# Ordering a four-direction scan kernel by pairs of units: one joined ssm_out, W ahead of the projections, c*h on GpSimd

## The chip, the cores and the metric

One core of a Trainium2 chip runs the whole program. The metric is the device time of one execution in microseconds (us). The engines are named as the profile names them: PE is TensorE's matmuls, PEld its weight loads, DVE VectorE, ACT ScalarE, POOL GpSimd.

## The reference, cut to what matters

An image batch (4, 128, 96, 96) is normalised by groups, read in four directions (rows, columns, each forwards and backwards), and each direction runs this block in fp32:

```python
t = _grouped1x1(x, in_proj_w, in_proj_b, G)
u, gate = (t[:, :HID], t[:, HID:])
u = jax.nn.silu(u)
u = lax.conv_general_dilated(u, dw_w, ...)          # depthwise, 5 taps
s = _conv1x1(u, ssm_in_w)
a = DMIN + (DMAX - DMIN) * jax.nn.sigmoid(_conv1x1(u, ssm_delta_w, ssm_delta_b))
a = jnp.clip(a, 0.0001, 0.9999)
bb = jnp.tanh(_conv1x1(u, ssm_b_w, ssm_b_b))
cc = jnp.tanh(_conv1x1(u, ssm_c_w, ssm_c_b))
prefix = jnp.cumsum(jnp.log(a), axis=-1)
hst = jnp.exp(prefix) * jnp.cumsum(bb * s * jnp.exp(-prefix), axis=-1)
u = u + _conv1x1(cc * hst + ssm_d[None, :, None] * s, ssm_out_w)
u = _grouped1x1(u * jax.nn.sigmoid(gate), mix_w, mix_b, G)
return _conv1x1(u, out_proj_w, out_proj_b)          # then the fuse of four directions, x +
```

The kernel computes `hst` as a first-order scan h = a*h + b*s. It folds mix, out_proj and fuse into one matrix, called W below.

## The kernel before

A *unit* is 384 positions of one stream; the two streams (a direction and its reverse) alternate, so two consecutive units are a *pair*. There are 384 units, 192 pairs. The last stages of a unit run 12 units behind its first ones. The names used below: *rows* are the in-projection matmuls (front `pf` and gate `pg`), *conv* `pc`, *projections* `pp`, *ssm_out* `pz`, *W* `py`. Two more names occur in the profiles: `gv` is the tile that W reads, and *gating* the two VectorE instructions that make it out of ssm_out and the gate; *bn_stats* collects the statistics of the next image.

```python
banks = []
w, x, y, z, h = range(5)
for _ in range(NU // 2 + 16):                      # PSUM banks rotate from unit to unit
    banks.append({"f": (w, x), "g": (y, z), "y": y, "c": (z, None), "t": h})
    banks.append({"f": (w, x), "g": (z, y), "y": h, "c": (z, y), "t": None})
    w, x, y, z, h = x, h, z, y, w
# ... in rows(), behind the 16 front and gate matmuls of a unit:
pz = ps.tile([P, 2, 512], F32, tag="z", name=f"pz_{bu['id']}")
for c in range(4):
    for j in range(2):                             # 8 tiles of 32x32: this unit's stream alone
        r = slice(64 * j + 32 * bu["s"], 64 * j + 32 * bu["s"] + 32)
        mm(pz[:, j, :], c, w_so[r, ...], z[r, bu["p"], :], True, True)
# ...
def outputs(step, p):
    ta, tb = scans[step]
    nc.vector.tensor_mul(tb[0:64, p, :], tb[0:64, p, :], ta[0:64, p, :])     # c*h
    nc.vector.tensor_add(tb[64:P, p, :], tb[0:64, p, :], tb[64:P, p, :])     # z
    nc.gpsimd.tensor_copy(tb[0:64, p, :], tb[64:P, p, :])                    # its copy
# ... the order on TensorE within unit(t):
#   rows (16 tiles), ssm_out (8), W of the unit before, conv (1 or 2), projections
```

Of the kernel before, what the change touches and what calls it, by code (L numbers as in the profile page):

```python
# [48 lines left out]
LAG = 12  # L49
# [4 lines left out]
def conv_preact_kernel(  # L54
# [58 lines left out]
    def psb(bank, name):  # L113
        return ps.tile([P, 512], F32, tag=f"bank{bank}", name=name)



    banks = []
    w, x, y, z, h = range(5)
    for _ in range(NU // 2 + 16):  # L120
        banks.append({"f": (w, x), "g": (y, z), "y": y, "c": (z, None), "t": h})
        banks.append({"f": (w, x), "g": (z, y), "y": h, "c": (z, y), "t": None})
        w, x, y, z, h = x, h, z, y, w
# [39 lines left out]
    def stats_finish(b):  # L163
# [4 lines left out]
        pm = ps.tile([P, 512], F32, tag="p", name=f"pm_{b}")  # L168
# [10 lines left out]
        pv = ps.tile([P, 512], F32, tag="p", name=f"pv_{b}")  # L179
# [7 lines left out]
        pb = ps.tile([P, 512], F32, tag="p", name=f"pbn_{b}")  # L187
# [65 lines left out]
    with tc.tile_pool(name="prep", bufs=1) as pp:  # L253
# [31 lines left out]
        for d in range(4):  # L285
            for j in range(2):
                pt = psb(2 * (d % 2) + j, f"pof_{d}_{j}")
                nc.tensor.matmul(
                    pt[:, :P], w_out[:, bass.ts(j, P)], w_fuse[:, d, :], start=True, stop=True
                )  # L290
                nc.scalar.copy(w_of[:, d, j, :], pt[:, :P])
        for d in range(4):
            for j in range(2):
                pt = psb(2 * (d % 2) + j, f"pfin_{d}_{j}")
# [4 lines left out]
        pb = psb(4, "pb")  # L299
# [21 lines left out]
    def gating(bu):  # L321
        gv = bu["v"]
        nc.vector.scalar_tensor_tensor(gv, gv, 1.0, bu["pz"][:, :, :N], ALU.add, ALU.mult)  # L323

# [5 lines left out]
    def rows(i, bi, bk):  # L330

        front = gate = None
        if i is not None:
# [9 lines left out]
            pf = [psb(bk["f"][j], f"pf_{i}_{j}") for j in range(2)]  # L343
            front = (un, wn, bsil, s, g, sil, pf)
        if bi is not None:
            bu = units[bi]
            gwn, gbn, _ = stats[bu["b"]]
            pg = [psb(bk["g"][j], f"pg_{bu['id']}_{j}") for j in range(2)]
            gate = (bu, gwn, gbn, pg)
        so = bu["s"] if gate else 0  # L350
        for e in (so, 1 - so):
            r, rg = slice(32 * e, 32 * e + 32), slice(64 + 32 * e, 96 + 32 * e)
            for c in range(4):
                if front:
                    m, q = (c, g) if by_taps(s, e) else (g, c)
                    mm(pf[e], c, wn[r, 32 * m : 32 * m + 32], x_in[s][r, q, :], True, True)
                if gate:
                    q, off = gate_at(bu)
                    mm(pg[e], c, gwn[rg, 32 * c : 32 * c + 32],
                       x_in[bu["s"]][rg, q, off : off + N], True, True)  # L360
        if gate:
            pz = ps.tile([P, 2, 512], F32, tag="z", name=f"pz_{bu['id']}")
            z = scans[bu["step"]][1]
            for c in range(4):
                for j in range(2):
                    r = slice(64 * j + 32 * bu["s"], 64 * j + 32 * bu["s"] + 32)
                    mm(pz[:, j, :], c, w_so[r, 128 * j + 32 * c : 128 * j + 32 * c + 32],
                       z[r, bu["p"], :], True, True)
        if gate:
            gv = wk.tile([P, 2, N], F32, tag="gv", name=f"gv_{bu['id']}")  # L370
            for j in range(2):
                nc.scalar.activation(  # L372
                    gv[:, j, :], pg[j][:, :N], AF.Tanh, bias=gbn[:, 2 + j : 3 + j], scale=0.5
                )
            load_gate(bi + UB)
            nc.vector.tensor_add(pz[:, :, :N], pz[:, :, :N], bu["u"])  # L376
            bu["pz"], bu["v"] = pz, gv
        if front:
            for j in range(2):
                nc.scalar.activation(  # L380
                    sil[:, j, g, :],
                    pf[j][:, : N + 1],
# [3 lines left out]
            if g == 3:  # L386
                for j in range(2):
                    if un["st"] == 0:
# [18 lines left out]
    def taps(un, ks, bk):  # L407
        sil, j = sils[un["step"], un["s"]], 1
        if 0 in ks:
            un["pt"] = psb(bk["t"], f"pt_{un['id']}")  # L410
# [229 lines left out]
```

## Time and profile before

| | before |
|---|---|
| median of 3 runs | 2586.16 us (2585.37 to 2586.33) |
| busy PE, DVE, ACT, POOL | 98%, 78%, 60%, 20% of 2589.8 us |
| one pair in mid-kernel | 12.90 us, 36 slots of 0.3225 us and 1.29 us of other time |
| ahead of the first ssm_out, and from the last one's start to the end | 99.9 and 10.4 us |

Read the busy shares as a list of engines that cannot be the bound, not as a measure of TensorE. PE's 98% includes time in which tiles drain or start late, and those 1.29 us per pair are as much a target as the slots are. The lines that carry this are in the prediction.

### The profile page before, as it was taken

To read this page: it belongs to the slowest core of one execution; us is meant where nothing else is said; L and a number is where in the kernel's file an instruction comes from. 1 tells how busy PE (TensorE), PEld (TensorE's weight loads), DVE (VectorE), ACT (ScalarE), POOL (GpSimd) and SP (SyncE) were. 2 spreads that over 40 slices of the span, in tenths; PEclk is the share of its full clock that TensorE was granted. 3 is DMA by queue.
4 is the path that set the end of the run, shared out by engine and by line. 5 is a ranking of instruction groups with operands and counts; after the bars stand their busy time and mean duration, and the time that the engine had idled before them with its cause. 6 is when DMAs were issued, how large, how long until landed. Compare 5 with 4: busy or idle time off the path is not lost.

```text
span 2589.8 us, 89224 instructions
## 1 busy us (share of the span) xinstructions
PE 2534.8 (98%) x40016; PEld 964.0 (37%) x40016; DVE 2023.1 (78%) x2727; ACT 1554.8 (60%) x2912; POOL 512.2 (20%) x786
## 2 busy tenths in 40 slices
PE   6999999999999999999999999999999999999997
PEld 3333333333333333333333333333333333333332
DVE  3688878877878887877887887777887788778876
ACT  4666666666656666666665666666666666666652
POOL 4211121111111112111111111211111111111110
PEclk8999999999999999999999999999999999999999
DMA  5112111112332111111232211111133111111111
GB/s 141 46 45 51 45 37 30 36 30 84 94 92 51 45 48 28 36 30 36 81 112 81 51 45 31 36 30 36 30 101 110 36 30 36 29 36 30 29 42 58
DMA packets 79278, 134.18 MB, mean 52 GB/s; under 512 B 11440, under 2 KB 73392, under 8 KB 78896
## 3 DMA queue, kind: packets, MB, share of 16 engines
q1 hardware_dynamic: 76704, 127.64, 18.4%
q8 instruction: 315, 5.16, 0.8%
q10 hardware_dynamic: 2192, 0.83, 0.1%
q14 instruction: 67, 0.55, 0.1%
HBM read 109.55 MB, written 18.87 MB: 50 GB/s over the span
## 4 chain that ended last, share of the span: by engine, by line
PE 95%; DVE 1%; ACT 1%; DMA 1%; issue 0%; DVEq 0%; ACTq 0%
PE pc L317 29%; PE py L317 21%; PE pp L317 20%; PE pz L317 12%; PE pf L317 11%; PE pg L317 2%; DVE gv L323 0%; DVE t L479 0%; DMA out<-acc 0%; ACT t L445 0%; DMA acc<-in_xr 0%; ACT gv L372 0%; DMA x_in<-in_xs 0%; ACT L445 0%; ACT L182 0%
## 5 line engine op out<-in xcount | busy, mean ns | idle before, releaser
L317 PE MATMUL pc<-sil,band 128*32 128x384 f32 x9216 | 822.1, 489 | 0.3 <-ACT gv L372 0.3
L402 ACT COPY u<-pc 128x384 f32<-128x384 f32 x576 | 276.2, 479 | 568.3 <-PE pc L317 567.0
L317 PE MATMUL pp<-u,w_proj 128*32 128x384 f32 x6144 | 596.0, 489 | 7.1 <-ACT std L182 5.6
L317 PE MATMUL py<-gv,w_fin 128*32 128x384 f32 x6144 | 580.0, 495 | 6.2 <-ACT gv L372 4.2
L417 DVE SCALAR_TENSOR_TENSOR pt<-sil,w_tap,pt 128x384 f32<-128x384 f32 x576 | 358.5, 622 | 180.9 <-ACT pt L415 165.8
L317 PEld LDWEIGHTS pc<-sil,band 128*32 128x32 f32 x9216 | 297.4, 110 | 457.6 <-issue 388.9
L372 ACT ACTIVATE gv<-pg,bnorm 128x384 f32<-128x384 f32 x768 | 403.1, 576 | 97.3 <-PE pg L317 97.3
L317 PE MATMUL pz<-t,w_so 32*32 32x384 f32 x6144 | 430.7, 492 | 5.6 <-DVE gv L323 5.5
L459 DVE TENSOR_TENSOR t<-pp,t 64x384 f32<-64x384 f32 x192 | 176.2, 918 | 286.9 <-ACT t L451 286.8
L376 DVE TENSOR_TENSOR pz<-pz,u 128x768 f32<-128x768 f32 x384 | 369.8, 963 | 14.4 <-PE pz L317 8.5
L317 PE MATMUL pf<-x_in,wn 32*32 32x385 f32 x6144 | 362.6, 504 | 8.2 <-DVE acc L504 7.2
L317 PE MATMUL pg<-x_in,wn 32*32 32x384 f32 x6144 | 360.2, 494 | 3.4 <-DVE acc L511 3.4
L323 DVE SCALAR_TENSOR_TENSOR gv<-gv,pz 128x768 f32<-128x768 f32 x384 | 362.6, 944 | 0.1
L448 POOL TENSOR_SCALAR t<-t 64x384 f32<-64x384 f32 x192 | 184.0, 958 | 858.9 <-ACT t L445 858.9
L317 PEld LDWEIGHTS pp<-u,w_proj 128*32 128x32 f32 x6144 | 224.7, 109 | 304.4 <-issue 259.8
L487 POOL COPY t<-t 64x384 f32<-64x384 f32 x192 | 96.3, 501 | 1156.7 <-DVE t L486 1156.7
L380 ACT ACTIVATE sil<-pf,bsilu 128x385 f32<-128x385 f32 x576 | 314.6, 586 | 3.9 <-PE pf L317 3.3
L317 PEld LDWEIGHTS py<-gv,w_fin 128*32 128x32 f32 x6144 | 160.7, 109 | 397.1 <-issue 270.2
L451 ACT ACTIVATE t<-pp,b_proj 64x384 f32<-64x384 f32 x192 | 110.6, 576 | 242.6 <-PE pp L317 122.4
L445 ACT ACTIVATE t<-pp,b_proj 128x384 f32<-128x384 f32 x192 | 187.0, 974 | 70.2 <-PE pp L317 53.8
L317 PEld LDWEIGHTS pz<-t,w_so 32*32 32x32 f32 x6144 | 167.1, 103 | 165.2 <-issue 91.7
L449 POOL TENSOR_SCALAR t<-t 64x384 f32<-64x384 f32 x192 | 184.8, 962 | 15.9
(65 smaller groups left out, 1474.0 us busy)
## 6 DMA issues: line engine op xcount, KB each, us to landing
x_in<-in_xs SPq DMA_DIRECT2D x96, 385.0 KB, 4.3
x_in<-in_xs SPq DMA_DIRECT2D x384, 96.2 KB, 2.4
out<-acc SPq DMA_DIRECT2D x24, 768.0 KB, 3.6
xs<-in_xr SPq DMA_DIRECT2D x72, 192.0 KB, 2.4
acc<-in_xr SPq DMA_DIRECT2D x18, 768.0 KB, 4.7
acc<-in_xr SPq DMA_DIRECT2D x24, 192.0 KB, 3.6
w_fuse<-in_fuse_wT ACTq DMA_DIRECT2D x1, 256.0 KB, 4.9
w_proj<-in_proj_wT ACTq DMA_DIRECT2D x1, 128.0 KB, 4.6
```

What stands on the lines that cost most here:

```text
L317: nc.tensor.matmul(o[r, : rhs.shape[-1]], lhsT, rhs, start=start, stop=stop, skip_group_check=True)
L323: nc.vector.scalar_tensor_tensor(gv, gv, 1.0, bu["pz"][:, :, :N], ALU.add, ALU.mult)
L372: nc.scalar.activation(gv[:, j, :], pg[j][:, :N], AF.Tanh, bias=gbn[:, 2 + j : 3 + j], scale=0.5)
L376: nc.vector.tensor_add(pz[:, :, :N], pz[:, :, :N], bu["u"])
L380: nc.scalar.activation(sil[:, j, g, :], pf[j][:, : N + 1], AF.Silu, bias=bn[:, j : j + 1] if by_taps(s, j) else bsil[:, j, g : g + 1],)
L402: nc.scalar.copy(un["u"][:, j, :], pc[:, :N])
L417: nc.vector.scalar_tensor_tensor(un["u"][:, j, :] if k == K - 1 else part, src, w_tap[:, k : k + 1], part, ALU.mult, ALU.add,)
L445: nc.scalar.activation(ta[:, p, :], pp[:, :N], AF.Tanh, bias=b_proj[:, 0:1])
L448: nc.gpsimd.tensor_scalar(a, a, half, DMIN + half, ALU.mult, ALU.add)
L449: nc.gpsimd.tensor_scalar(a, a, 0.9999, 0.0001, ALU.min, ALU.max)
L451: nc.scalar.activation(tb[0:64, p, :], pp[0:64, :N], AF.Tanh, bias=b_proj[0:64, 1:2])
L459: nc.vector.tensor_mul(ta[0:64, p, :], pp[64:P, :N], ta[0:64, p, :])
```

## The change

The intent: the 32x32 matmuls of ssm_out used two of the four row groups of the array, one stream at a time. Taking both streams of a pair together fills all four. To make that possible all work is ordered by pairs, PSUM banks become fixed, W of the even unit moves between convolution and projections, and c*h and z go to GpSimd. The diff cut to its core:

```diff
-    for _ in range(NU // 2 + 16):
-        banks.append({"f": (w, x), "g": (y, z), "y": y, "c": (z, None), "t": h})
...
+    psum = ps.tile([P, 8, 512], F32, name="psum")
+    GATE, FRONT, CONV_R, Y_F, SMALL = (0, 1), (2, 3), (0, 1), 2, 3
+    SSM, PROJ, Y_R, CONV_F = (4, 6), (5, 4), 6, 7
...
+    def ssm_out(bi):
+        pair = units[bi], units[bi + 1]
+        z, p = scans[pair[0]["step"]][1], pair[0]["p"]
+        for c in range(4):
+            for s in range(2):
+                for j in range(2):
+                    r = slice(64 * j + 32 * s, 64 * j + 32 * s + 32)
+                    mm(bank(SSM[s] + j), c, w_so[r, ...], z[r, p, :], True, True)
+        for s, bu in enumerate(pair):
+            pz, gv = psum[:, SSM[s] : SSM[s] + 2, :N], bu["v"]
+            nc.vector.tensor_add(pz, pz, bu["u"])
+            nc.vector.scalar_tensor_tensor(gv, gv, 1.0, pz, ALU.add, ALU.mult)
...
-        nc.vector.tensor_mul(tb[0:64, p, :], tb[0:64, p, :], ta[0:64, p, :])
-        nc.vector.tensor_add(tb[64:P, p, :], tb[0:64, p, :], tb[64:P, p, :])
+        nc.gpsimd.tensor_mul(ta[64:P, p, :], tb[0:64, p, :], ta[0:64, p, :])
+        nc.gpsimd.tensor_add(tb[64:P, p, :], ta[64:P, p, :], tb[64:P, p, :])
         nc.gpsimd.tensor_copy(tb[0:64, p, :], tb[64:P, p, :])
...
+    def pair(t):             # order on TensorE, shortened
+        inputs(i - 2); rows(front, bi); accumulate(units[bi - 1]); conv(units[i], 0)
+        scan(...); outputs(...)
+        rows(front + 1, bi + 1); ssm_out(bi); conv(units[i + 1], 0 and 1)
+        accumulate(units[bi]); taps(units[i + 2], range(K)); proj(i, 1); proj(i, 0)
```

`accumulate` is W. `inputs` is the tanh of the first projection, GpSimd's two clamping operations and the product b*s. The taps, the convolution of one half of the channels done on VectorE, now accumulate in u itself instead of a PSUM bank.

More of the change, by code (lines that the diff above doesn't have):

```diff
@@ L48 @@
 M = WW // R
-LAG = 12
+LAG = 6
 UB = 8
@@ L111, in conv_preact_kernel, with bank @@
     NU = len(units)
-    def psb(bank, name):
-        return ps.tile([P, 512], F32, tag=f"bank{bank}", name=name)
-    banks = []
-    w, x, y, z, h = range(5)
-    for _ in range(NU // 2 + 16):
-        banks.append({"f": (w, x), "g": (y, z), "y": y, "c": (z, None), "t": h})
-        banks.append({"f": (w, x), "g": (z, y), "y": h, "c": (z, y), "t": None})
-        w, x, y, z, h = x, h, z, y, w
+    psum = ps.tile([P, 8, 512], F32, name="psum")
+    GATE, FRONT, CONV_R, Y_F, SMALL = (0, 1), (2, 3), (0, 1), 2, 3
+    SSM, PROJ, Y_R, CONV_F = (4, 6), (5, 4), 6, 7
+    def bank(i):
+        return psum[:, i, :]
     gmean = wp.tile([P, P], F32, name="gmean")
@@ L167, in stats_finish @@
         yield
-        pm = ps.tile([P, 512], F32, tag="p", name=f"pm_{b}")
+        pm = bank(SMALL)
         nc.tensor.matmul(pm[:, 0:1], gmean, mv[:, 0:1], start=True, stop=True)
@@ L178, in stats_finish @@
         yield
-        pv = ps.tile([P, 512], F32, tag="p", name=f"pv_{b}")
+        pv = bank(SMALL)
         nc.tensor.matmul(pv[:, 0:1], gmean, ex, start=True, stop=True)
@@ L186, in stats_finish @@
         yield
-        pb = ps.tile([P, 512], F32, tag="p", name=f"pbn_{b}")
+        pb = bank(SMALL)
         nc.tensor.matmul(pb[:, 0:4], wn, gm4, start=True, stop=True)
@@ L286, in conv_preact_kernel @@
             for j in range(2):
-                pt = psb(2 * (d % 2) + j, f"pof_{d}_{j}")
+                pt = bank(2 * (d % 4) + j)
                 nc.tensor.matmul(
@@ L293, in conv_preact_kernel @@
             for j in range(2):
-                pt = psb(2 * (d % 2) + j, f"pfin_{d}_{j}")
+                pt = bank(2 * (d % 4) + j)
                 nc.tensor.matmul(
@@ L298, in conv_preact_kernel @@
                 nc.scalar.mul(w_fin[:, d, j, :], pt[:, :P], 0.5)
-        pb = psb(4, "pb")
+        pb = bank(0)
         terms = [(w_of[:, d, j, :], b_mix[:, j : j + 1]) for d in range(4) for j in range(2)]
@@ L318, in mm @@
                          skip_group_check=True)
-    def gating(bu):
-        gv = bu["v"]
-        nc.vector.scalar_tensor_tensor(gv, gv, 1.0, bu["pz"][:, :, :N], ALU.add, ALU.mult)
     def by_taps(s, j):
@@ L328, in conv_preact_kernel, with rows @@
     sils = {}
-    def rows(i, bi, bk):
-        front = gate = None
+    def rows(i, bi, front_banks=FRONT):
         if i is not None:
@@ L342, in rows @@
             sil = sils[step, s]
-            pf = [psb(bk["f"][j], f"pf_{i}_{j}") for j in range(2)]
-            front = (un, wn, bsil, s, g, sil, pf)
         if bi is not None:
@@ L347, in rows @@
             gwn, gbn, _ = stats[bu["b"]]
-            pg = [psb(bk["g"][j], f"pg_{bu['id']}_{j}") for j in range(2)]
-            gate = (bu, gwn, gbn, pg)
-        so = bu["s"] if gate else 0
-        for e in (so, 1 - so):
-            r, rg = slice(32 * e, 32 * e + 32), slice(64 + 32 * e, 96 + 32 * e)
-            for c in range(4):
-                if front:
-                    m, q = (c, g) if by_taps(s, e) else (g, c)
-                    mm(pf[e], c, wn[r, 32 * m : 32 * m + 32], x_in[s][r, q, :], True, True)
-                if gate:
-                    q, off = gate_at(bu)
-                    mm(pg[e], c, gwn[rg, 32 * c : 32 * c + 32],
-                       x_in[bu["s"]][rg, q, off : off + N], True, True)
-        if gate:
-            pz = ps.tile([P, 2, 512], F32, tag="z", name=f"pz_{bu['id']}")
-            z = scans[bu["step"]][1]
-            for c in range(4):
-                for j in range(2):
-                    r = slice(64 * j + 32 * bu["s"], 64 * j + 32 * bu["s"] + 32)
-                    mm(pz[:, j, :], c, w_so[r, 128 * j + 32 * c : 128 * j + 32 * c + 32],
-                       z[r, bu["p"], :], True, True)
-        if gate:
+            gq, off = gate_at(bu)
+        for c in range(4):
+            for j in range(2):
+                if i is not None:
+                    r = slice(32 * j, 32 * j + 32)
+                    m, q = (c, g) if by_taps(s, j) else (g, c)
+                    mm(bank(front_banks[j]), c, wn[r, 32 * m : 32 * m + 32], x_in[s][r, q, :],
+                       True, True)
+                if bi is not None:
+                    r = slice(64 + 32 * j, 96 + 32 * j)
+                    mm(bank(GATE[j]), c, gwn[r, 32 * c : 32 * c + 32],
+                       x_in[bu["s"]][r, gq, off : off + N], True, True)
+        if bi is not None:
             gv = wk.tile([P, 2, N], F32, tag="gv", name=f"gv_{bu['id']}")
@@ L372, in rows @@
                 nc.scalar.activation(
-                    gv[:, j, :], pg[j][:, :N], AF.Tanh, bias=gbn[:, 2 + j : 3 + j], scale=0.5
+                    gv[:, j, :],
+                    bank(GATE[j])[:, :N],
+                    AF.Tanh,
+                    bias=gbn[:, 2 + j : 3 + j],
+                    scale=0.5,
                 )
             load_gate(bi + UB)
-            nc.vector.tensor_add(pz[:, :, :N], pz[:, :, :N], bu["u"])
-            bu["pz"], bu["v"] = pz, gv
-        if front:
+            bu["v"] = gv
+        if i is not None:
             for j in range(2):
@@ L381, in rows @@
                     sil[:, j, g, :],
-                    pf[j][:, : N + 1],
+                    bank(front_banks[j])[:, : N + 1],
                     AF.Silu,
@@ L387, in rows, with conv @@
                 for j in range(2):
+                    tap = by_taps(s, j)
                     if un["st"] == 0:
-                        r = (slice(0, P), slice(0, 2)) if by_taps(s, j) else (slice(0, 64), slice(0, 4))
-                        nc.gpsimd.memset(sil[r[0], j, r[1], 0:1], 0.0)
+                        r, q = (slice(0, P), slice(0, 2)) if tap else (slice(0, 64), slice(0, 4))
+                        nc.gpsimd.memset(sil[r, j, q, 0:1], 0.0)
                     if un["st"] == NS - 1:
-                        r = (slice(0, P), slice(2, 4)) if by_taps(s, j) else (slice(64, P), slice(0, 4))
-                        nc.gpsimd.memset(sil[r[0], j, r[1], N : N + 1], 0.0)
+                        r, q = (slice(0, P), slice(2, 4)) if tap else (slice(64, P), slice(0, 4))
+                        nc.gpsimd.memset(sil[r, j, q, N : N + 1], 0.0)
                 load_front(step + 1, s)
-    def conv(un, j, bk):
+    def ssm_out(bi):
+        pair = units[bi], units[bi + 1]
+        z, p = scans[pair[0]["step"]][1], pair[0]["p"]
+        for c in range(4):
+            for s in range(2):
+                for j in range(2):
+                    r = slice(64 * j + 32 * s, 64 * j + 32 * s + 32)
+                    mm(bank(SSM[s] + j), c, w_so[r, 128 * j + 32 * c : 128 * j + 32 * c + 32],
+                       z[r, p, :], True, True)
+        for s, bu in enumerate(pair):
+            pz, gv = psum[:, SSM[s] : SSM[s] + 2, :N], bu["v"]
+            nc.vector.tensor_add(pz, pz, bu["u"])
+            nc.vector.scalar_tensor_tensor(gv, gv, 1.0, pz, ALU.add, ALU.mult)
+    def conv(un, j):
         sil = sils[un["step"], un["s"]]
-        pc = psb(bk["c"][j], f"pc_{un['id']}_{j}")
+        pc = bank(CONV_R[j] if un["s"] else CONV_F)
         for k in range(2):
@@ L404, in new_u, with taps @@
     def new_u(un):
-        un["u"] = wk.tile([P, 2, N], F32, tag="u", bufs=LAG + 1, name=f"u_{un['id']}")
-    def taps(un, ks, bk):
+        un["u"] = wk.tile([P, 2, N], F32, tag="u", bufs=2 * LAG + 2, name=f"u_{un['id']}")
+    def taps(un, ks):
         sil, j = sils[un["step"], un["s"]], 1
-        if 0 in ks:
-            un["pt"] = psb(bk["t"], f"pt_{un['id']}")
         for k in ks:
             off, q = divmod(un["p"] + k, R)
-            src, part = sil[:, j, q, off : off + N], un["pt"][:, :N]
+            src, part = sil[:, j, q, off : off + N], un["u"][:, j, :]
             if k == 0:
@@ L417, in taps @@
                 nc.vector.scalar_tensor_tensor(
-                    un["u"][:, j, :] if k == K - 1 else part,
-                    src,
-                    w_tap[:, k : k + 1],
-                    part,
-                    ALU.mult,
-                    ALU.add,
+                    part, src, w_tap[:, k : k + 1], part, ALU.mult, ALU.add
                 )
@@ L435, in proj @@
                 wk.tile([P, N, R], F32, tag="t0", name=f"t0_{step}").rearrange("p n r -> p r n"),
-                wk.tile([P, R, N], F32, tag="t1", name=f"t1_{step}"),
+                wk.tile([P, R, N], F32, tag="t1", bufs=3, name=f"t1_{step}"),
             ]
         ta, tb = scans[step]
-        pp = ps.tile([P, 512], F32, tag="p", name=f"pp_{un['id']}_{which}")
+        pp = bank(PROJ[which])
         cols = (qb, qb, qa, qa) if which == 0 else (qc, qc, qs, qs)
@@ L443, in proj @@
                 mm(pp, c, w_proj[:, j, cols[c]], units[i + c % 2]["u"][:, j, :], j == 0, j == 1)
-        if which == 0:
-            nc.scalar.activation(ta[:, p, :], pp[:, :N], AF.Tanh, bias=b_proj[:, 0:1])
-            a = ta[64:P, p, :]
-            half = (DMAX - DMIN) / 2
-            nc.gpsimd.tensor_scalar(a, a, half, DMIN + half, ALU.mult, ALU.add)
-            nc.gpsimd.tensor_scalar(a, a, 0.9999, 0.0001, ALU.min, ALU.max)
-        else:
+        if which == 1:
             nc.scalar.activation(
@@ L453, in proj, with inputs @@
             )
-            un["pp"] = pp
-    def products(i):
+            nc.scalar.activation(tb[64:P, p, :], pp[64:P, :N], AF.Copy, scale=d_sb[64:P, :])
+    def inputs(i):
         un = units[i]
-        (ta, tb), p, pp = scans[un["step"]], un["p"], un["pp"]
-        nc.vector.tensor_mul(ta[0:64, p, :], pp[64:P, :N], ta[0:64, p, :])
-    def skip(i):
-        un = units[i]
-        tb = scans[un["step"]][1]
-        nc.scalar.activation(
-            tb[64:P, un["p"], :], un["pp"][64:P, :N], AF.Copy, scale=d_sb[64:P, :]
-        )
+        ta, p = scans[un["step"]][0], un["p"]
+        nc.scalar.activation(ta[:, p, :], bank(PROJ[0])[:, :N], AF.Tanh, bias=b_proj[:, 0:1])
+        a = ta[64:P, p, :]
+        half = (DMAX - DMIN) / 2
+        nc.gpsimd.tensor_scalar(a, a, half, DMIN + half, ALU.mult, ALU.add)
+        nc.gpsimd.tensor_scalar(a, a, 0.9999, 0.0001, ALU.min, ALU.max)
+        nc.vector.tensor_mul(ta[0:64, p, :], bank(PROJ[1])[64:P, :N], ta[0:64, p, :])
     def scan(step, part):
@@ L484, in outputs, with accumulate @@
         ta, tb = scans[step]
-        nc.vector.tensor_mul(tb[0:64, p, :], tb[0:64, p, :], ta[0:64, p, :])
-        nc.vector.tensor_add(tb[64:P, p, :], tb[0:64, p, :], tb[64:P, p, :])
+        nc.gpsimd.tensor_mul(ta[64:P, p, :], tb[0:64, p, :], ta[0:64, p, :])
+        nc.gpsimd.tensor_add(tb[64:P, p, :], ta[64:P, p, :], tb[64:P, p, :])
         nc.gpsimd.tensor_copy(tb[0:64, p, :], tb[64:P, p, :])
-    def accumulate(bu, bk):
+    def accumulate(bu):
         b, s, p, st = bu["b"], bu["s"], bu["p"], bu["st"]
-        py = psb(bk["y"], f"py_{bu['id']}")
+        py = bank(Y_R if s else Y_F)
         for j in range(2):
@@ L519, in conv_preact_kernel @@
     later = []
-    def unit(t):
-        bi, k, bk = t - LAG, t % UB, banks[t]
-        un = units[t] if t < NU else None
-        if t % 2 and 0 <= t - 3 < NU:
-            products(t - 3)
-        if t % 2 and 0 <= t - 11 < NU:
-            d = units[t - 11]
-            outputs(d["step"], d["p"])
-        if un and k % 2 == 0:
-            taps(un, range(1, K), bk)
-        rows(t + UB if t + UB < NU else None, bi if 0 <= bi < NU else None, bk)
-        if t % 2 and 0 <= t - 3 < NU:
-            skip(t - 3)
-        if 0 <= bi - 1 < NU:
-            accumulate(units[bi - 1], bk)
-        if 0 <= bi < NU:
-            gating(units[bi])
-        if un:
-            conv(un, 0, bk)
-            if k % 2:
-                conv(un, 1, bk)
+    def pair(t):
+        i, k, bi = 2 * t, t % R, 2 * (t - LAG)
+        conv_here = i < NU
+        front = i + UB if i + UB < NU else None
+        back = 0 <= bi < NU
+        if 0 <= i - 2 < NU:
+            inputs(i - 2)
+        rows(front, bi if back else None)
+        if 0 <= bi - 2 < NU:
+            accumulate(units[bi - 1])
+        if conv_here:
+            conv(units[i], 0)
+        if k < 2 and 0 <= t // R - 1 < NU // UB:
+            scan(t // R - 1, k)
+        if 0 <= i - 10 < NU:
+            d = units[i - 10]
+            outputs(d["step"], d["p"])
+        if conv_here:
+            un = units[i]
+            if un["order"] == "V" and un["b"] + 1 < B:
+                stats_chunk(un["b"] + 1, un["st"] * R + k)
+                if un["st"] == NS - 1 and k == R - 1:
+                    later[:] = [stats_finish(un["b"] + 1)]
+        if front is not None or back:
+            rows(None if front is None else front + 1, bi + 1 if back else None)
+        if back:
+            ssm_out(bi)
+        if conv_here:
+            new_u(units[i + 1])
+            for j in range(2):
+                conv(units[i + 1], j)
+        if back:
+            accumulate(units[bi])
@@ L542, in unit @@
         if later:
             next(later[0], None)
-        if un and un["order"] == "V" and k % 2 == 0 and un["b"] + 1 < B:
-            stats_chunk(un["b"] + 1, (un["st"] * UB + k) // 2)
-            if un["st"] == NS - 1 and k == UB - 2:
-                later[:] = [stats_finish(un["b"] + 1)]
-        if k in (1, 2) and 0 <= t // UB - 1 < NU // UB:
-            scan(t // UB - 1, k - 1)
-        if t + 1 < NU:
-            new_u(units[t + 1])
-            if k % 2:
-                taps(units[t + 1], [0], banks[t + 1])
@@ L554, in unit @@
-        if k % 2 and un:
-            proj(t - 1, 0)
-        elif k % 2 == 0 and 2 <= t <= NU:
-            proj(t - 2, 1)
+        if i + 2 < NU:
+            new_u(units[i + 2])
+            taps(units[i + 2], range(K))
+        if conv_here:
+            proj(i, 1)
+            proj(i, 0)
     for _ in stats_finish(b0):
@@ L561, in conv_preact_kernel @@
     for i in range(UB):
-        r = 2 * (i % 2)
-        rows(i, None, {"f": (r, r + 1)})
+        rows(i, None, (2 * (i % 2), 2 * (i % 2) + 1))
     new_u(units[0])
-    taps(units[0], [0], banks[0])
+    taps(units[0], range(K))
     with tc.manual_schedule(
@@ L568, in conv_preact_kernel @@
     ):
-        for t in range(NU + LAG + 1):
-            unit(t)
+        for t in range(NU // 2 + LAG + 1):
+            pair(t)
 _NAMES = [
```

## The prediction

> **What bounds the kernel now.** I read the page's busy times first, then the chain of work that ended last, then the groups of lines, and only then the timeline, because "98% busy" on TensorE does not say whether its time is streaming, switching or waiting.
>
> ```profile
> PE 2534.8 (98%) x40016; PEld 964.0 (37%) x40016; DVE 2023.1 (78%) x2727; ACT 1554.8 (60%) x2912; POOL 512.2 (20%) x786
> ...
> PE pc L317 29%; PE py L317 21%; PE pp L317 20%; PE pz L317 12%; PE pf L317 11%; PE pg L317 2%; DVE gv L323 0%; DVE t L479 0%; DMA out<-acc 0%; ACT t L445 0%; DMA acc<-in_xr 0%; ACT gv L372 0%; DMA x_in<-in_xs 0%; ACT L445 0%; ACT L182 0%
> ...
> L317 PE MATMUL pz<-t,w_so 32*32 32x384 f32 x6144 | 430.7, 492 | 5.6 <-DVE gv L323 5.5
> L376 DVE TENSOR_TENSOR pz<-pz,u 128x768 f32<-128x768 f32 x384 | 369.8, 963 | 14.4 <-PE pz L317 8.5
> L317 PE MATMUL pf<-x_in,wn 32*32 32x385 f32 x6144 | 362.6, 504 | 8.2 <-DVE acc L504 7.2
> ```
>
> The chain is matmuls from end to end: TensorE's own order sets the time, and no other engine is above 78%. The counts show that each fp32 matmul is recorded as two passes (6144 = 192 pairs x 16 matmuls x 2). The timeline of TensorE's weight loads in mid-kernel shows how a pass is paced:
>
> ```profile
> 1304.47 0.11 PEld L317 LDWEIGHTS pp<-u,w_proj 128*32 128x32 f32 x1 [0.19 <-issue]
> 1304.79 0.28 PEld L317 LDWEIGHTS pp<-u,w_proj 128*32 128x32 f32 x7 [0.21 <-issue]
> ...
> 1306.05 0.10 PEld L317 LDWEIGHTS pz<-t,w_so 32*32 32x32 f32 x1
> 1306.37 0.42 PEld L317 LDWEIGHTS pz<-t,w_so 32*32 32x32 f32 x15 [0.22 <-issue]
> 1307.42 0.16 PEld L317 LDWEIGHTS py<-gv,w_fin 128*32 128x32 f32 x8 [0.62 <-ACT gv L372]
> 1307.77 0.13 PEld L317 LDWEIGHTS py<-gv,w_fin 128*32 128x32 f32 x4 [0.19 <-issue]
> 1308.09 0.13 PEld L317 LDWEIGHTS py<-gv,w_fin 128*32 128x32 f32 x4 [0.19 <-issue]
> 1308.41 0.13 PEld L317 LDWEIGHTS pc<-sil,band 128*32 128x32 f32 x4 [0.19 <-issue]
> ```
>
> Four column tiles start together and the next four follow 0.323 us later. I call that a slot; a slot costs the same whether 4, 8 or 16 tiles share it. The matmul rows of the same stretch:
>
> ```profile
> 1304.14 1.63 PE L317 MATMUL pp<-u,w_proj 128*32 128x384 f32 x16
> 1305.70 0.51 PE L317 MATMUL pf<-x_in,wn 32*32 32x385 f32 x1
> 1305.70 0.51 PE L317 MATMUL pg<-x_in,wn 32*32 32x384 f32 x1
> ...
> 1306.15 0.48 PE L317 MATMUL pg<-x_in,wn 32*32 32x384 f32 x1
> 1306.37 1.12 PE L317 MATMUL pz<-t,w_so 32*32 32x384 f32 x16
> 1307.42 1.50 PE L317 MATMUL py<-gv,w_fin 128*32 128x384 f32 x16
> ```
>
> pz (ssm_out) ends at 1307.49, so its last matmul of 0.48 started at 1307.01 and W (py) came 0.41 later. pp's last start (1305.28) to pf is 0.42. So a change between 32-row and 128-row tiles costs 0.41 after the last start, about 0.09 more than a slot. And pz occupies 1306.37 to 1307.42, 1.05 us for two slots of work (0.65): its first tile starts on time, the other loads come later and spread.
>
> Two units repeat every 12.90 us: rows start at 1305.70, 1311.43 and 1318.60 (5.73 + 7.17). Slots in that: conv 12, projections 8, W 8, pz 4, rows 4 = 36, times 0.3225 = 11.61. The other 1.29 us: two rows-pz-W passages at 0.40 each, two entries to rows 0.11 and 0.27, two rows passes 0.03 each. The 0.27 comes from the odd unit's projection, one load at 1304.79 while the rest wait for ScalarE's copy of u.
>
> **What the Trainium skill says.** "TensorEngine Tiling (Array Packing)", Key Properties, says that a change of tiling mode drains TensorE; the trace agrees, 0.41 us from last start to first start. Its table of 32x32 tiles has 16 positions; old pz uses 8 at a time, rows use 16 at the price of one slot. "GPSIMD Engine Reference", 3.1, gives a GpSimd tensor_tensor of 2048 fp32 4497 ns, and section 7 adds half for steps over 8 bytes. No GpSimd tensor_tensor is in this trace. "SBUF — State Buffer", Who interferes with whom, says a VectorE instruction with two SBUF inputs contends with GpSimd reads. The trace shows it:
>
> ```profile
> 353.52 1.81 DVE L479 TENSOR_TENSOR_SCAN t<-t 64x768 f32<-64x768 f32 x1
> 353.59 5.46 POOL L195 COPY bsilu<-bnorm 32x2 f32<-32x2 f32 x15
> ```
>
> These copies have a mean of 284 ns; 15 of them are 4.3 us, but took 5.46 beside the scan.
>
> **The change, part by part, per pair of units on TensorE.**
>
> 1. ssm_out once per pair on all four row groups: 4 slots become 2. Removed 2 x 0.3225 = 0.645. This is not all gain: rows to pz to W now occurs once. Today it takes 1.37 us from the rows' second pass to W, twice = 2.74. After, the first rows of the pair go straight to W: 16 starts spread over 0.10, then 0.41 = 0.51. The second rows go to ssm_out with 16 tiles instead of 8. The trace's loads of pz fill 0.42 us for 15, of which the second part is spread at about 17 ns a tile; eight more tiles add 0.13, so 1.37 + 0.13 = 1.50. Sum 2.01: saved 0.73. If the tiles go out at the rows' rate (7 ns) it is 1.36 and the saving 0.87.
> 2. W of the even unit between convolution and projections: 4 slots = 1.29 us in which ScalarE's copy (0.48) finishes. The stall of the odd projection goes: 0.27 - 0.11 = 0.16.
> 3. The number of mode changes stays four per pair (rows to W, conv to rows, ssm_out to conv, projection to rows).
>
> Sum 0.73 + 0.16 = 0.89, with the favourable rate 1.03; by adding up afresh: 34 slots = 10.97, rows 0.05, rows to W 0.19, rows to ssm_out to conv 0.53, two entries 0.22 = 11.96 (or 11.82). I take 11.93. 192 pairs x (12.90 - 11.93) = 186 us.
>
> 4. c*h and z leave VectorE: 192 x (909 + 555 ns) = 281 us, 1.46 per pair. VectorE falls from about 2023 to 1742, 9.1 of 11.9 us per pair. It is not on the chain, so this buys only slack, but slack that is needed: both gatings now come together after one ssm_out.
> 5. GpSimd gains 192 x 2 operations. Estimate from the skill's page: 4497/2048 = 2.2 ns x 384 = 0.84, half more for the strided scan tile = 1.26 us each. 512 + 192 x 2.5 = 992 us, 5 of 11.9 us per pair: no bound. A pair's z is made one pair before ssm_out reads it.
> 6. Taps accumulate in u (SBUF) instead of PSUM. The same 622 ns expected.
>
> **Do the other engines keep up?** From the start R of a pair's first rows: ScalarE's tanh starts 0.13 after R (1305.83), gate tanh at 0.98, Silu at 1.92, done 2.98 (1308.68). The second rows need those banks at 0.84 + W 1.29 + conv 1.29 + 0.11 = R + 3.53; margin 0.5. ssm_out ends near R + 5.4. VectorE then needs 0.99 + 0.86 (starts at 1303.36, 1304.35; 1304.89, 1305.75) for the first gating, so gv is ready at 7.4; W wants it at 5.35 + 8 slots = 7.93. Margin 0.5. The second gating is done at 9.3, W of it is due at 12.8. Taps (4 x 0.64) after the accumulation end at about 12.6, 0.7 into the next pair; its products at 1.1 to 2.1, accumulation to 2.9, and where there is a scan, GpSimd's clamps end at 3.2 and the scan at 5.0, before ssm_out's end.
>
> Head, tail and batch changes: 2589.8 - 192 x 12.90 = 113 us. Same lag (12 units = 6 pairs), same reloads of the accumulator, so I leave them, less a few us in the head.
>
> **Rivals.** (a) VectorE becomes late in the pairs with a scan: GpSimd starts c*h just when the scan wants the shared read port, the scan waits up to 1.3 us, gating slips past the 0.5 us margin, and TensorE waits for gv. One pair in four, up to 0.8 us: 48 x 0.8 = 38 us, total about 2440. For it: bsilu's case above; against it: the ordering lets the scan start second only by 0.1 us, and most pairs have slack. (b) Fixed PSUM banks take the place of rotation: bank 2 serves rows and even W, banks 0 and 1 gate and convolution. Any lateness of ScalarE or VectorE then stops rows at once. A loss of 0.5 us in each pair makes 2500. Against: every margin I found is 0.2 us or more, and the waits show ScalarE's copy of u waiting 567 us in all for TensorE, not the reverse. (c) The passage into 16 tiles of ssm_out is no cheaper than two of 8, as starts are issued serially: then only parts 2 and the single drain remain, 0.3 us per pair, about 2530. The rows' 16 starts within 0.11 us speak against it. (d) GpSimd so slow that z comes late: it would need over 5 us more per pair than estimated.
>
> **Range and chances.** 2586 - 186 = 2400, plus about 8 us for scan pairs (a quarter of rival a): 2408 us. Low end: 7 ns rate and shorter tail, 2586 - 1.09 x 192 = 2377, less a little. High end: rivals a and a part of b, 2465. Faster by over 2% is below 2534: only rival c in full or b with two thirds of a microsecond per pair prevents it. Faster 0.94, within 2% 0.05, slower 0.01.
>
> **What would show it.** Right: TensorE still over 95% busy, rows repeating every 11.8 to 12.0 us per pair, ssm_out's busy time near 192 x 1.25 = 240 us instead of 431 (its 1.12 per unit plus 0.13 for the wider set, once per pair), no wait of TensorE on ScalarE in the projections, VectorE near 1740 us, GpSimd near 1000. Wrong: periods alternating with the scan pairs, W waiting for VectorE's gv, rows waiting for Silu or for acc, or ssm_out lasting over 1.3 us.

## The result, and the profile after

| | before | after |
|---|---|---|
| median, 4 runs each | 2586.24 us | 2461.41 us (2459.89 to 2466.89) |
| ratio | | 0.9522, 95% interval 0.9505 to 0.9538 |
| busy PE, DVE, ACT, POOL in us | 2535, 2023, 1555, 512 | 2389, 1859, 1573, 1051 |

A ratio here is the mean time of one kernel's fast runs over the mean of the other's of the same rounds, so it is not quite the ratio of the medians. The change is faster by 4.8%. The time lies inside the predicted range, 53 us above its centre.

The page of the changed kernel, with the lines that answer to those of before. All matmul outputs are now called psum, so the stage is read from the inputs: t is ssm_out, gv is W, x_in the rows. The numbers behind the bar are busy us, mean ns, and idle time ahead with what ended it.

```profile
PE psum L314 82%; DVE t L465 4%; ACT t L447 2%; DVE gv L394 2%; DVE psum L393 2%; POOL t L450 1%; POOL t L451 1%; DVE u L415 0%; DMA out<-acc 0%; DVE bn L310 0%; DMA acc<-in_xr 0%; ACT gv L353 0%; ACT L364 0%; ACT L438 0%; ACT sil L364 0%
...
L314 PE MATMUL psum<-gv,w_fin 128*32 128x384 f32 x6144 | 582.9, 497 | 31.0 <-DVE gv L394 29.0
...
L472 POOL TENSOR_TENSOR t<-t,t 64x384 f32<-64x384 f32 x192 | 289.1, 1506 | 15.0
L471 POOL TENSOR_TENSOR t<-t,t 64x384 f32<-64x384 f32 x192 | 249.5, 1300 | 95.9 <-DVE t L465 85.9
L314 PE MATMUL psum<-t,w_so 32*32 32x384 f32 x6144 | 256.2, 493 | 2.9 <-DVE t L452 2.9
```

Three things stand in it. ssm_out went from 430.7 us to 256.2, near the 240 expected. The chain is no longer TensorE from end to end: 4% of it is the scan (L465), and the two gating lines (L393, L394) and GpSimd's clamps are in it too. And W now waits for gv, 29 us by this count.

TensorE's timeline in the changed kernel, one whole pair without a wait (columns: start, duration, engine, line, operation):

```profile
1326.67 0.94 PE L314 MATMUL psum<-x_in,wn 32*32 32x385 f32 x32
1327.54 1.51 PE L314 MATMUL psum<-gv,w_fin 128*32 128x384 f32 x16
1328.85 1.49 PE L314 MATMUL psum<-sil,band 128*32 128x384 f32 x16
1330.27 0.93 PE L314 MATMUL psum<-x_in,wn 32*32 32x385 f32 x32
1330.94 1.30 PE L314 MATMUL psum<-t,w_so 32*32 32x384 f32 x32
1332.17 2.79 PE L314 MATMUL psum<-sil,band 128*32 128x384 f32 x32
1334.78 1.47 PE L314 MATMUL psum<-gv,w_fin 128*32 128x384 f32 x16
1336.07 2.77 PE L314 MATMUL psum<-u,w_proj 128*32 128x384 f32 x32
1338.76 0.94 PE L314 MATMUL psum<-x_in,wn 32*32 32x385 f32 x32
```

Subtract starts, not ends: ends are modelled and overlap. Rows to rows is 1338.76 - 1326.67 = 12.09 us against 12.90. The first rows reach W in 0.87, the second rows pass ssm_out and reach the convolution in 1.90: 2.77, where the kernel before needed 2 x 1.72 = 3.44. Projections to rows is 2.69, 8 slots and 0.11.

But one pair in four is longer. The starts of ssm_out put the pairs at a median of 12.06 to 12.09 us, except those that hold the first half of a scan, at 12.52 (mean 12.60, some at 12.97). Here is one of the longest kind on TensorE:

```profile
1319.19 2.79 PE L314 MATMUL psum<-sil,band 128*32 128x384 f32 x32
1322.66 1.50 PE L314 MATMUL psum<-gv,w_fin 128*32 128x384 f32 x16 [0.69 <-DVE gv L394]
```

The conv takes 2.61 us without a wait; here W starts 3.47 after it, because gv is not there. VectorE and GpSimd at that time:

```profile
1317.06 2.93 DVE L465 TENSOR_TENSOR_SCAN t<-t,t 64x768 f32<-64x768 f32 x1 [0.36 <-POOL t L451]
1320.03 0.56 DVE L310 BATCH_NORM_STATS2 bn<-xs 128x6 f32<-128x384 f32 x1
...
1321.56 0.95 DVE L394 SCALAR_TENSOR_TENSOR gv<-gv,psum 128x768 f32<-128x768 f32 x1
```

```profile
1317.11 1.28 POOL L471 TENSOR_TENSOR t<-t,t 64x384 f32<-64x384 f32 x1
1318.47 2.54 POOL L472 TENSOR_TENSOR t<-t,t 64x384 f32<-64x384 f32 x1
```

The scan took 2.93 us instead of 1.81. It lies beside c*h (L471), which began as its clamps ended, and z (L472) is then stretched to 2.54 and ends 1.0 us after the scan. The gating is ready at 1322.51, and W starts 0.15 later.

The same trace holds a control. Most first-half scans take over a carried value (t<-t,t); those that begin a new sequence do not (t<-t). In seven of the latter c*h starts just as close behind the scan, but there c*h is the one that is stretched, and the scan is not:

```profile
375.68 1.75 DVE L465 TENSOR_TENSOR_SCAN t<-t 64x768 f32<-64x768 f32 x1 [0.37 <-POOL t L451]
```

```profile
375.73 2.76 POOL L471 TENSOR_TENSOR t<-t,t 64x384 f32<-64x384 f32 x1
```

These seven pairs lasted 12.06 us, like pairs without such a scan. Where the scan was stretched, the pairs without bn_stats behind it have a median of 12.50 us, the 14 with it 12.97.

### The profile page after: what moved, and what is told of

The parts are those of the page before. It is cut to its first block, busy times and chain, and to the rows that moved or that the text cites. A ratio compares the mean times of both kernels' runs of the same rounds, so it can differ in the third digit from the quotient of the medians.

```text
span 2461.1 us, 89876 instructions
## 1 busy us (share of the span) xinstructions
PE 2389.1 (97%) x40016; PEld 913.3 (37%) x40016; DVE 1859.2 (76%) x2343; ACT 1572.8 (64%) x2912; POOL 1051.3 (43%) x1170
## 4 chain that ended last, share of the span: by engine, by line
PE 82%; DVE 9%; POOL 3%; ACT 3%; issue 1%; DMA 0%; DVEq 0%; SPq 0%
PE psum L314 82%; DVE t L465 4%; ACT t L447 2%; DVE gv L394 2%; DVE psum L393 2%; POOL t L450 1%; POOL t L451 1%; DVE u L415 0%; DMA out<-acc 0%; DVE bn L310 0%; DMA acc<-in_xr 0%; ACT gv L353 0%; ACT L364 0%; ACT L438 0%; ACT sil L364 0%
## 5 line engine op out<-in xcount | busy, mean ns | idle before, releaser
L314 PE MATMUL psum<-sil,band 128*32 128x384 f32 x9216 | 821.6, 488 | 0.0
L314 PE MATMUL psum<-gv,w_fin 128*32 128x384 f32 x6144 | 582.9, 497 | 31.0 <-DVE gv L394 29.0
L393 DVE TENSOR_TENSOR psum<-psum,u 128x768 f32<-128x768 f32 x384 | 369.3, 962 | 248.3 <-PE psum L314 247.5
L314 PE MATMUL psum<-u,w_proj 128*32 128x384 f32 x6144 | 533.0, 486 | 0.0
L415 DVE SCALAR_TENSOR_TENSOR u<-sil,w_tap,u 128x384 f32<-128x384 f32 x768 | 478.9, 624 | 56.9 <-ACT u L413 35.7
L353 ACT ACTIVATE gv<-psum,bnorm 128x384 f32<-128x384 f32 x768 | 403.7, 577 | 153.2 <-PE psum L314 153.2
L314 PE MATMUL psum<-x_in,wn 32*32 32x385 f32 (+1 forms) x12288 | 389.9, 502 | 13.3 <-DVE acc L490 8.5
L394 DVE SCALAR_TENSOR_TENSOR gv<-gv,psum 128x768 f32<-128x768 f32 x384 | 366.5, 955 | 43.7 <-ACT sil L364 0.9
L364 ACT ACTIVATE sil<-psum,bsilu 128x385 f32<-128x385 f32 x576 | 314.6, 586 | 5.6 <-PE psum L314 5.4
L472 POOL TENSOR_TENSOR t<-t,t 64x384 f32<-64x384 f32 x192 | 289.1, 1506 | 15.0
L471 POOL TENSOR_TENSOR t<-t,t 64x384 f32<-64x384 f32 x192 | 249.5, 1300 | 95.9 <-DVE t L465 85.9
L314 PE MATMUL psum<-t,w_so 32*32 32x384 f32 x6144 | 256.2, 493 | 2.9 <-DVE t L452 2.9
```

Of the source, the lines that this page charges most:

```text
L314: nc.tensor.matmul(o[r, : rhs.shape[-1]], lhsT, rhs, start=start, stop=stop, skip_group_check=True)
L353: nc.scalar.activation(gv[:, j, :], bank(GATE[j])[:, :N], AF.Tanh, bias=gbn[:, 2 + j : 3 + j], scale=0.5,)
L364: nc.scalar.activation(sil[:, j, g, :], bank(front_banks[j])[:, : N + 1], AF.Silu, bias=bn[:, j : j + 1] if by_taps(s, j) else bsil[:, j, ...
L393: nc.vector.tensor_add(pz, pz, bu["u"])
L394: nc.vector.scalar_tensor_tensor(gv, gv, 1.0, pz, ALU.add, ALU.mult)
L415: nc.vector.scalar_tensor_tensor(part, src, w_tap[:, k : k + 1], part, ALU.mult, ALU.add)
```

## The experiments

The theory after the result: TensorE's order still sets the time, in pairs of 12.08 us; what came out above 2408 us is the collision of scan and c*h, a slightly longer pair than added up, and the tail. Rivals: the gain came from freeing VectorE, not from the joined ssm_out; or the scan pairs are long merely because VectorE has more to do in them. Seven kernels ran, all with correct results. Their ratios are to the kernel before in their own rounds; in the rounds of the first four it had a median of 2594.06 us, in those of the last three 2587.16 us. The kernel before varied more than the others (2585.07 to 2596.15 us in the first of these rounds), so a difference taken from two ratios can differ by several us from one taken from two medians; both are given where it matters.

| kernel | median us | ratio (95% interval) |
|---|---|---|
| changed kernel, first runs | 2461.41 | 0.9522 (0.9505 to 0.9538) |
| changed kernel, again | 2463.72 | 0.9512 (0.9485 to 0.9539) |
| c*h and z on VectorE | 2512.13 | 0.9693 (0.9674 to 0.9712) |
| ssm_out by stream | 2539.75 | 0.9799 (0.9778 to 0.9819) |
| even W behind the projections | 2478.18 | 0.9561 (0.9540 to 0.9582) |
| c*h behind the scan | 2437.17 | 0.9402 (0.9383 to 0.9421) |
| that, and the tail by stream | 2425.62 | 0.9365 (0.9339 to 0.9392) |
| before, c*h on GpSimd alone | 2582.99 | 0.9967 (0.9933 to 1.0002) |

**c*h and z given back to VectorE** (in the changed kernel)

```diff
-        nc.gpsimd.tensor_mul(ta[64:P, p, :], tb[0:64, p, :], ta[0:64, p, :])
-        nc.gpsimd.tensor_add(tb[64:P, p, :], ta[64:P, p, :], tb[64:P, p, :])
+        nc.vector.tensor_mul(tb[0:64, p, :], tb[0:64, p, :], ta[0:64, p, :])
+        nc.vector.tensor_add(tb[64:P, p, :], tb[0:64, p, :], tb[64:P, p, :])
```

> The changed kernel with c*h and z given back to VectorE (only the copy stays on GpSimd). Theory: TensorE's order sets the time, so moving these off VectorE gained little; it even costs time in the pairs with a scan, where GpSimd's c*h and the scan overlap (scan 2.93 us in place of 1.81). Then this kernel is within 1% of the changed kernel: 2450 to 2485 us, the scan is back at 1.81 us, VectorE's busy time rises by about 280 us, and some lateness of the gating appears in the pairs with c*h behind a scan. Rival: freeing VectorE was the gain; then this kernel goes back towards 2586 us, by 60 us or more.

It cost 1.8% (0.9693 / 0.9522), some 44 us (51 by the medians): between the two expectations, so my figure was too small. The scan of the first half was back at 1.81 us, as expected. VectorE's timeline shows what takes its place:

```profile
1343.90 1.81 DVE L465 TENSOR_TENSOR_SCAN t<-t,t 64x768 f32<-64x768 f32 x1 [0.35 <-POOL t L451]
1345.75 0.88 DVE L471 TENSOR_TENSOR t<-t,t 64x384 f32<-64x384 f32 x1
...
1348.79 0.95 DVE L394 SCALAR_TENSOR_TENSOR gv<-gv,psum 128x768 f32<-128x768 f32 x1
```

c*h and z stand between the scan and the gating. gv is ready at 1349.74 and TensorE's W starts at 1349.89, 3.86 us after the start of its convolution at 1346.03. Now both pairs with a scan are long (medians 12.82 and 12.58 us) and the other two are not. So lost slack on VectorE had a price in two pairs of four, although the engine was only 84% busy on average.

**ssm_out by stream**

```diff
-    def ssm_out(bi):
+    def ssm_out(bi, streams):
...
-            for s in range(2):
+            for s in streams:
...
+            ssm_out(bi, (0,))
             rows(None if front is None else front + 1, bi + 1 if back else None)
-            ssm_out(bi)
+            ssm_out(bi, (1,))
```

> The changed kernel with ssm_out in two sets of 8 tiles again, the even stream's ahead of the second rows and the odd stream's behind them; all else the same. Theory: joining the sets is the main gain, two slots and a staggered start per pair; undone it costs 0.6 to 0.8 us per pair, 115 to 155 us: 2575 to 2615 us, and the pair repeats every 12.7 to 12.9 us. Rival: the tiles of both sets overlap anyway, or the gain came from the place of W and the freed VectorE: then it stays below 2500 us.

It went to 2539.75 us. Ratios put it 2.9% above the changed kernel, some 72 us (78 by the medians), less than the 115 to 155 I expected. Yet the pair without a wait repeats every 12.67 us, 0.59 more than 12.08 and near the expected 0.6 to 0.8. TensorE's timeline:

```profile
1364.43 0.55 PE L314 MATMUL psum<-t,w_so 32*32 32x384 f32 x8
1364.50 0.55 PE L314 MATMUL psum<-x_in,wn 32*32 32x385 f32 x4
...
1365.93 0.93 PE L314 MATMUL psum<-t,w_so 32*32 32x384 f32 x15
1366.92 2.79 PE L314 MATMUL psum<-sil,band 128*32 128x384 f32 x32
```

Set of 8, rows, set of 8 take 1366.92 - 1364.43 = 2.49 us where rows and the joined set take 1.90. The first set and the rows even overlap: rows start 0.07 us after the set, one matmul of which lasts 0.5. The difference is the 0.59 x 192 = 113 us. Against it stands what the split gives back: the even stream's gating no longer waits for both streams, so the scan pairs are no longer long (their medians are those of the other pairs, although c*h still stretches the scan, to a median of 2.86 us), and the tail pairs took 8.84 us in place of 10.54. Joining is the main gain, but it also delays the first gating.

**The even unit's W behind the projections**

```diff
+    Y_F = 7
...
-        if back:
-            accumulate(units[bi])
         if later:
             next(later[0], None)
...
             proj(i, 1)
             proj(i, 0)
+        if back:
+            accumulate(units[bi])
```

> The changed kernel with W of the even unit behind the projections (its output in bank 7, so that the first rows need not wait for it). Theory: the projections then wait again for ScalarE's copy of u, 0.16 us per pair, 31 us in all: 2485 to 2500 us, with a wait of the projections' weight loads on ScalarE's copy in the list of waits. Rival: 4 slots are 4 slots wherever they stand, and the copy is hidden by the first half of the projection: 2461 us within 5 us. A second effect works the other way: W then waits less for gv in the scan pairs, worth up to 21 us.

The ratio rose by 0.4%, about 10 us (17 by the medians): more than the rival allowed, less than I expected. The pair without a wait took 12.21 to 12.24 us: 0.15 more, as the theory had it (0.16). The old sign of the late copy is back in the weight loads of the projections, one load on time and the others behind:

```profile
1315.96 0.11 PEld L315 LDWEIGHTS psum<-u,w_proj 128*32 128x32 f32 x1 [0.19 <-issue]
1316.28 1.57 PEld L315 LDWEIGHTS psum<-u,w_proj 128*32 128x32 f32 x23 [0.21 <-issue]
```

That wait did not appear in the list of waits, where I had looked for it: the lag is carried on and is paid on the way into the rows, 0.27 us instead of 0.11. The total is smaller than 31 us since the scan pairs are no longer than others here (the second effect), while the tail pairs took 13.2 us.

**c*h behind the scan**

```diff
             d = units[i - 10]
+            if k == 0 and t // R - 1 < NU // UB:
+                hint = wk.tile([P, 1], F32, tag="hint", name=f"hint_{t}")
+                nc.gpsimd.tensor_copy(
+                    hint[0:64, :], scans[t // R - 1][0][0:64, R - 1, N // 2 - 1 : N // 2]
+                )
             outputs(d["step"], d["p"])
```

> The changed kernel with one tiny GpSimd copy of the first half scan's last output ahead of c*h, in the one pair of four whose first half scan runs: so GpSimd's c*h begins after the scan instead of beside it. Theory: the 0.45 to 0.9 us by which these pairs are longer (12.5 to 12.97 us against 12.08) are the scan held up by c*h on the shared read port, and TensorE's W waiting for gv behind it; they go, the scan is back near 1.81 us, and the time falls by 20 to 30 us to 2432 to 2445 us. Rival: these pairs are longer because VectorE has a scan and bn_stats more to do at all: then the time stays within 5 us of 2461.

2437.17 us, 1.3% below the changed kernel by ratio, some 31 us, and 24 us by the medians: as the theory had it (20 to 30). VectorE in such a pair:

```profile
1302.37 1.81 DVE L465 TENSOR_TENSOR_SCAN t<-t,t 64x768 f32<-64x768 f32 x1 [0.37 <-POOL t L451]
1304.21 0.56 DVE L310 BATCH_NORM_STATS2 bn<-xs 128x6 f32<-128x384 f32 x1
```

The scan is back at 1.81, although VectorE has just as much to do, bn_stats included, and these pairs have the median 12.06 us of the others. So the collision, not the amount of VectorE's work, made them long; the seven pairs above, with a scan that was not stretched, say the same. bn_stats adds its part only where the scan is already late.

**The tail by stream, on top of it**

```diff
+        tail = back and not conv_here
+        if tail:
+            ssm_out(bi, (0,))
         rows(...)
-            ssm_out(bi)
+            ssm_out(bi, (1,) if tail else (0, 1))
```

> The kernel with c*h behind the scan, and in the last pairs alone, where there is no convolution to hide the gating, ssm_out goes by stream (8 tiles, rows, 8 tiles). Theory: the tail lost time because W of the even unit stands right behind the joined ssm_out and waits for the gating (10.5 us per tail pair against 8.8 with ssm_out by stream): 5 or 6 pairs save 1.7 us each, 8 to 11 us, the ratio to the kernel before falls from 0.940 to 0.936. Rival: the chain through VectorE in the tail is the same length either way: no change.

2425.62 us, the fastest of all; its ratio is 0.4% below that of the kernel without the tail's edit, as expected. The two were not run in the same rounds and their intervals just overlap; the trace is the better evidence: the last five pairs took 8.4 us each instead of 10.3, 9 us in all. The stretch table shows a second possible cause that I had not named. Its columns are the stretch, its length, busy time of the five engines, the granted clock of TensorE (the share of full speed that it was allowed), DMA share and GB/s. First the changed kernel, then this one, each in mid-kernel and in the tail:

```profile
2300.00:2390.00 90.00, 89.56 (x1425) 33.86 (x1418) 70.22 (x86) 51.55 (x95) 39.19 (x42) 1.00 0.12 36
2405.00:2450.00 45.00, 35.11 (x440) 9.56 (x432) 22.73 (x27) 9.72 (x19) 11.62 (x12) 0.73 0.11 41
```

```profile
2300.00:2370.00 70.00, 70.00 (x1093) 26.39 (x1083) 50.49 (x64) 38.55 (x71) 28.34 (x33) 1.00 0.13 41
2370.00:2415.00 45.00, 34.88 (x532) 11.13 (x512) 30.29 (x36) 11.58 (x22) 15.18 (x17) 0.85 0.12 44
```

In the tail TensorE waits for gv, and its granted clock falls to 0.73; with ssm_out by stream it holds 0.85. How much of the 10 us is the shorter chain and how much the clock is not separated here.

**c*h and z on GpSimd in the kernel before, nothing else**

```diff
-        nc.vector.tensor_mul(tb[0:64, p, :], tb[0:64, p, :], ta[0:64, p, :])
-        nc.vector.tensor_add(tb[64:P, p, :], tb[0:64, p, :], tb[64:P, p, :])
+        nc.gpsimd.tensor_mul(ta[64:P, p, :], tb[0:64, p, :], ta[0:64, p, :])
+        nc.gpsimd.tensor_add(tb[64:P, p, :], ta[64:P, p, :], tb[64:P, p, :])
```

> The kernel before with one part of the change alone: c*h and z on GpSimd, everything else as it was. Theory: in the kernel before TensorE's order sets the pair's 12.90 us and VectorE has slack everywhere, so freeing 1.46 us of VectorE per pair is worth nothing by itself: within 0.7% of 2586 us, VectorE's busy time down by about 280 us. It may lose up to 20 us where c*h and a scan meet. Rival: since giving c*h back to VectorE cost the changed kernel 1.7%, the move is worth as much here: 2545 us or less.

2582.99 us, ratio 0.9967 with an interval that just reaches 1: the same. VectorE fell from 2023 to 1783 us busy, and the pair stayed at 5.73 + 7.17 us. The same move is worth nothing in the old order and 1.8% in the new one. The scans here kept their 1.81 us: c*h was not next to them.

**The changed kernel again**

> The changed kernel itself once more, on this chip and in these rounds, as the base for the other runs: ratio to the kernel before 0.950 to 0.954.

0.9512, within the expected range: the base holds in these later rounds.

Taken back alone, the joined ssm_out costs 72 us, the place of W 10 and c*h on GpSimd 44, by ratios. That the sum, 126, meets the whole gain of 124 is partly chance, since the first two of these edits also removed the long scan pairs and changed the tail. The fixed banks, the order by pairs and the taps in u were not taken back alone.

## Why the prediction was right or wrong

The direction and the bound were right, the centre was 53 us too low. That the time still lies within the range, 4 us below its upper end, is partly luck: this end was drawn for rivals (a) and (b), while half of the excess came from a pair that the range took to be shorter, and (b) did not happen. Two of its signs of being wrong did appear, periods that follow the scan pairs and W waiting for gv, and the pair's 12.06 to 12.09 us lie outside its 11.8 to 12.0. By its own steps:

1. *ssm_out joined, 0.73 us per pair (0.87 if tiles start fast).* Measured 3.44 - 2.77 = 0.67. The slow rate was the true one: start times in the trace lie 17 ns apart for the 16 tiles, with 42 ns for the last two, which is the missing 0.05. The split experiment shows the step itself: 0.59 us per pair lost.
2. *W ahead of the projections, 0.16.* Right: the entry to the rows fell from 0.27 to 0.11, and moving W back cost 0.15.
3. *Four mode changes stay; the taps keep their length.* Right: a tap took 624 ns, 622 expected.
4. *The pair of 11.93.* This is the mis-sized term. It measured 12.08, and 0.15 x 192 = 29 us of the 53. Subtracting the steps from 12.90 had given 12.01; I let a fresh sum of slots (11.96) and the favourable rate pull it down. The fresh sum left out 0.05 us that the same sum also missed in the kernel before (it gave 12.85 of 12.90), so the difference of two measured pairs was the better ground.
5. *c*h and z on GpSimd "buys only slack, but slack that is needed".* Half right. Alone it buys nothing. In the new order it is worth some 44 us: on VectorE, c*h and z stand between the scan and the gating that W waits for. The estimate of 1.26 us per operation met 1.24 us (median of c*h); the means of 1.30 and 1.51 contain the collisions. VectorE's busy time ended at 1859 us, not 1742: the scans' own time grew by 51 us (173.3 to 224.2 us for the 96 of them), and the rest is that busy time counts overlapping instructions once. The instructions' own times summed to about 2121 us before (busy 2023) and to 1900 after (busy 1859), so fewer of them overlap.
6. *Rival (a), scan and c*h at the shared read port.* The stretched scan and the late gating came as described, and I gave them a quarter of their weight, 8 us; that the port is the reason no run here shows. It cost (12.60 - 12.08) x 46 pairs = 24 us, and putting c*h behind the scan gained 24 (medians) to 31 (ratios). This is 16 us of the 53. My example for it was misread, though not its direction: the mean of 284 ns contains the stretched copies. In the trace such a copy takes 0.18 us, and the one beside the scan took 1.72.
7. *Head and tail "left as they are".* The rest of about 8 us. The last pairs took 10.5 us each against 2 x 4.32 before: W stands right behind the joined ssm_out, with no convolution between to hide the gating. The tail experiment gives back 10 us. The 8 us are a net figure: in the profiled executions the last five pairs took 9 us more, the first ssm_out began 3.7 us later (103.6 against 99.9, where I had expected a few us less), and the other irregular pairs lay some 20 us above the order's pace, against 32 before.
8. *Rivals (b) and (c).* Fixed banks did not stop the rows: pairs without a scan run at the order's own pace. Starts are indeed issued serially, as (c) feared, but at 17 ns, too little to undo the gain.

## What to carry to other kernels

When one engine's order is the bound, add up its steps from start to start, and take a change's gain as a difference between measured passages; a sum built afresh inherits what you forgot. Joining small matmuls over all row groups paid here, but the work that follows then arrives at once, so check the engine behind it in its worst pair, not in its average. And when work moves to GpSimd, look at which VectorE instruction with two SBUF inputs it will start beside: one tiny dependency that sets the order was worth a fifth to a quarter of the whole gain.

## What the Trainium skill lacked or had wrong

- "TensorEngine Tiling (Array Packing)", Key Properties, has only a change of mode drain the array. Here ssm_out follows the rows in the same 32x32 mode, and its first tile starts on time, but its second starts 0.41 us after the last start of the rows, as after a change of mode (start times in the trace: 1330.72 and 1331.13). Why is open.
- "TensorE: Matmul & The Clock Gate", Measured speedup vs the span model, gives about 4 ns per tile. The rows' tiles start 7 ns apart, those of ssm_out 17 ns, with two gaps of 42 ns.
- "SBUF — State Buffer", Who interferes with whom, has issue order, not the shape of the operation, decide which engine is held up. By recorded starts c*h came 0.04 to 0.05 us after the scan in all 47 cases, and yet the loser differed: the 40 scans with a carried value were stretched (in the pair shown 2.93 us instead of 1.81, while c*h kept 1.28 and z took 2.54 instead of about 1.23), but the seven without one kept 1.75, and c*h took 2.74 to 2.77 instead of 1.24. Recorded starts may not be the order in which the two asked for the port, so this does not refute the page; it shows that they do not tell who will wait.
- "GPSIMD Engine Reference", 3.1 and 7, has no figure for a strided tensor_tensor of this size. An estimate from its figures, 1.26 us for 384 fp32 with a stride of 16 bytes, met 1.24 us.
